# Scores in four row quarters, their banks shared with the products, and a rearranged order of work

## The chip, the cores and the metric

The kernel runs on one core of one Trainium2 chip. The metric is device time in microseconds for one execution of the whole program; lower is better. The engines are named as the profile names them: PE (TensorE matmuls) and PEld (its weight loads), DVE (VectorE), ACT (ScalarE), POOL (GpSimd) and SP (SyncE, which issues most DMAs).

## What is computed

The reference takes x of shape (4, 2048, 512) through four residual steps: a causal linear attention (layer a), a quantized product (ffn), a gated decaying recurrence (layer b), and the same ffn again. The change lies in layer b. Cut to what matters there:

```python
x = x + attn_a(layernorm(x))
x = x + ffn(layernorm(x))          # int8 levels of x and rhs, product, scales
x = x + attn_b(layernorm(x))
x = x + ffn(layernorm(x))

def attn_b(x):                     # 16 heads, rank 16, head width 32
    q, k, v = split(x @ q_w.T), split(x @ k_w.T), split(x @ v_w.T)
    q, k = rope(q), rope(k)
    q_r, k_r = q @ Wq, k @ Wk      # per head, 32 -> 16
    g = sigmoid(x @ g_w.T + g_b)
    # per step t: M = M * decay + outer(g_t * k_t * scale, v_t);  y_t = q_t @ M
    h = x + Y @ out_w.T + out_b
    return layernorm(h) * ln_g + ln_b
```

The recurrence is computed in chunks of 128 rows. Inside a chunk the outputs are masked scores (a product of decayed queries and keys) times v; what comes from earlier chunks goes through a stored state.

## The kernel before

Layer a comes first, and then layer b with the last ffn (`layer_b_mild`; the other branch is not taken with these inputs). Layer b walks over 32 blocks of 256 rows. A block has two rows of 128 tokens (index i) and two groups of eight heads (index g, 16 ranks for each head, so 128 partitions), which makes four chunks: chunk c is row c // 2, group c % 2.

The order of the work on PE, DVE, ACT and POOL is written out by hand in `blocks_of(n)`, under `tc.manual_schedule`: each engine runs its instructions in the order of the program. SP is not among these engines, so the order of its DMA queue is left to the framework. One call of `blocks_of(n)` interleaves four blocks: the chunks of block B (n), the products that prepare `after` (n + 1), the loading, normalization and turning of the rows of `later` (n + 2), and the output normalization and ffn of `before` (n - 1).

A chunk has two functions. `scores` (L1318) multiplies keys `k1` and queries `q1`: the 128 partitions are cut in two halves of 64 (four heads each), and each half gives a score bank of 128 x 512, four heads beside each other. The queries are laid out with one copy for each of the four heads, zero outside the head's own 16 partitions; ACT makes these copies in `prepare` (L1294) from `qs`. `scores` then issues the state's part of the outputs (`pyT`, L1333) and the masks (L1339), by which DVE copies the scores out of PSUM with the causal triangle. The second function holds `update` (`pub`, L1360, then `pairs` on DVE and the state on POOL) and `outputs` (`pyT`, L1373, and ACT's copy to `yT`).

The other functions that the change and the steps of the prediction touch:

- `features` (L1230) makes the rotated queries or keys of one group: 8 f32 products into `pr`, which DVE reads twice (`xc`, `xs`, L1238).
- `gates` (`pg`), `keys` (`pl`, L1263; then q by ACT, k by DVE) and `values` (`pvb`; the copy `vb` by ACT, L1212).
- `prepare`: on DVE `k1` (L1282; the page prints it as k) and `qs` (L1288), on ACT the head copies, on POOL `ke` and `q0` (L1298).
- `turn_keys`: `turn_halves` copies `ke` on DVE (`planes`, L710) and issues a DMA transpose from SP (L712). `turned_keys` joins the result on ACT (`kt`, L717).
- `norm_row` and `turn_row`: the same for the rows of a later block; `turn_row` has two POOL additions (L1205, L1206).
- `project` (`py`, L1394) and `weigh_output` (`h` by DVE at L1398, then statistics); `norm_output` (`h` at L131, then two POOL instructions).
- `levels` quantizes for the ffn; its product (`pf`, L681) is read by DVE (`f_y`, L683) and added by POOL (L684); `store` writes the block out.

PSUM has eight banks. In layer b they are handed out in rings, each used in turn:

```python
bank = banks(psum, mm=3, s=2, y=2, u=1)
```

"mm" serves pr, pg, pl, pvb, pf and py; "s" the scores. A tile that comes to a place in its ring waits until the last reader of the tile before it there is done. P is 128, TB 256, NTB 2, QB 128, NQ 1, R 16 and HG 8, so the loop over j in `scores` runs once.

Of the kernel before, what the change touches and what calls it, by code (L numbers as in the profile page):

```python
# [10 lines left out]
F32 = mybir.dt.float32  # L11
BF16 = mybir.dt.bfloat16
U16 = mybir.dt.uint16
AF = mybir.ActivationFunctionType
# [32 lines left out]
def hybrid_block_kernel(ctx: ExitStack, tc: tile.TileContext, t: dict, out: bass.AP):  # L47
# [588 lines left out]
    def run(steps):  # L636
        for f in steps:
            f()
# [432 lines left out]
    def layer_b_mild():  # L1071
        with ExitStack() as es:
# [4 lines left out]
            w = es.enter_context(tc.tile_pool(name="mb_w", bufs=1, reuse_waits="tile"))  # L1077
            pool = es.enter_context(tc.tile_pool(name="mb", bufs=2, reuse_waits="tile"))
            psum = es.enter_context(tc.tile_pool(name="mb_ps", bufs=1, space=PSUM, reuse_waits="tile"))

            bank = banks(psum, mm=3, s=2, y=2, u=1)
            at = [(b, blk) for b in range(NB) for blk in range(SEQ // TB)]

            def load_x(n):
# [23 lines left out]
            for name in ("b_gb", "b_decay", "head4", "diag", "causal"):  # L1108
# [167 lines left out]
            def prepare(B, g):  # L1276


                q, k = B.qk[g]
                A = Block()  # L1280
                A.k1 = pool.tile([P, NTB, NQ, P], F32, name=f"k1{g}", bufs=1)
                nc.vector.tensor_tensor(  # L1282
                    A.k1,
                    k.rearrange("p (i s) -> p i s", s=P).unsqueeze(2).to_broadcast([P, NTB, NQ, P]),
                    tk[:, g, :, :].unsqueeze(1).to_broadcast([P, NTB, NQ, P]), ALU.mult,
                )
                qs = pool.tile([P, NTB * NQ, QB], F32, name="qs", bufs=1)
                nc.vector.tensor_tensor(  # L1288
                    qs, q.rearrange("p (j s) -> p j s", s=QB),
                    tq[:, g, :].unsqueeze(1).to_broadcast([P, NTB * NQ, QB]), ALU.mult,  # L1290
                )
                A.q1 = pool.tile([P, NTB * NQ, 4, QB], F32, name=f"q1{g}", bufs=1)
                for h in range(4):
                    nc.scalar.activation(A.q1[:, :, h, :], qs, AF.Copy, scale=small["head4"][:, h : h + 1])  # L1294
# [18 lines left out]
            def chunk(B, i, g):  # L1313
# [4 lines left out]
                def scores():  # L1318


                    A = B.prep[g]
                    ps = [bank([P, NQ, 4, QB], F32, name="ps", tag="s") for _ in range(2)]
                    for j in range(NQ):
                        for half in range(2):
                            r = slice(half * 64, (half + 1) * 64)
                            nc.tensor.matmul(  # L1326
                                ps[half][:, j, :, :], A.k1[r, i, j, :], A.q1[r, NQ * i + j, :, :],
                                start=True, stop=True,
                            )
                    C.py = [bank([P, P], F32, name="pyT", tag="y") for _ in range(2)]  # L1330
                    for half in range(2):
                        r = slice(half * 64, (half + 1) * 64)
                        nc.tensor.matmul(  # L1333
                            C.py[half], st[r, half * P : (half + 1) * P], A.q0[r, i, :],
                            start=True, stop=False, skip_group_check=True,
                        )
                    C.a = pool.tile([P, 2, 4, P], F32, name="ab")
                    for half in range(2):
                        nc.vector.tensor_tensor(  # L1339
                            C.a[:, half, :, :].rearrange("p h (j s) -> p h j s", s=QB),  # L1340
                            ps[half].rearrange("p j h s -> p h j s"),
                            small["causal"].rearrange("p (j s) -> p j s", s=QB).unsqueeze(1)
                            .to_broadcast([P, 4, NQ, QB]),
                            ALU.mult,
                        )


# [20 lines left out]
                def outputs():  # L1368

                    for half in range(2):  # L1370
                        for h in range(4):
                            lo = g * HG * DB + (4 * half + h) * DB
                            nc.tensor.matmul(  # L1373
                                C.py[half][h * DB : (h + 1) * DB, :], B.v[:, i, lo : lo + DB],
                                C.a[:, half, h, :], start=False, stop=True, skip_group_check=True,
                            )
# [11 lines left out]
                return (lambda: (scores(), zero())) if ends else scores, lambda: run([outputs] if ends else [update, outputs])  # L1388

            def project(B, i):  # L1390

# [4 lines left out]
            def weigh_output(B, i):  # L1396
                h = B.h[i] = pool.tile([P, D], F32, name="h")
                nc.vector.tensor_tensor(h, B.py.pop(i), B.xr[:, i, :], ALU.add)  # L1398
                B.stats[i] = stats(pool, h.unsqueeze(1), 1)

            def norm_output(B, i):
                h, x = B.h.pop(i), B.x[:, i, :]
# [52 lines left out]
            def blocks_of(n):  # L1455
                B, after, later = blocks.get(n), blocks.get(n + 1), blocks.get(n + 2)
                before = blocks.get(n - 1)
                nothing = lambda: None
                chunks = [chunk(B, c // G, c % G) if B else (nothing, nothing) for c in range(2 * G)]


                if B:
                    turned_keys(B, 0)
                chunks[0][0]()
                if before:
                    weigh_ffn(before, 0)
                if after:
                    run(features(after, "q", 0))
                chunks[0][1]()
                if later:  # L1470
                    weigh_row(later, 0)
                if before:
# [8 lines left out]
                    turned_keys(B, 1)  # L1481
                chunks[1][0]()
                if before:
                    weigh_output(before, 1)
                if after:
                    run(gates(after, 0) + keys(after, 0))
                chunks[1][1]()
                if before:
                    run(before.levels[0])
                if later:  # L1490
# [3 lines left out]
                if later:  # L1494
                    weigh_row(later, 1)
                if after:
                    run(features(after, "q", 1))


                chunks[2][0]()  # L1500
                if after:
                    prepare(after, 0)
                if before:
                    weigh_ffn(before, 1)
                if later:
                    turn_row(later, 0)
                if after:
                    run(values(after, 0))
                    turn_keys(after, 0)
                chunks[2][1]()  # L1510
                if later:
                    norm_row(later, 1)
                if before:
                    levels(before, 1)
                if after:
# [25 lines left out]
            def tail(B):  # L1541
# [24 lines left out]

                project(B, 1)
                weigh_ffn(B, 0)
                weigh_output(B, 1)
                quantize(0)  # L1570
                norm_last(B, 1)
# [21 lines left out]
def _constants(seq):  # L1593
# [13 lines left out]
        "head4": (p[:, None] // R % 4 == np.arange(4)[None, :]).astype(f),  # L1607
# [89 lines left out]
```

## Time and profile before

| what | value |
|---|---|
| median of 3 runs | 3969.62 us (3968.38 to 3970.84) |
| the profiled execution, its own time | 3970.43 us |
| its span, first to last instruction | 3968.6 us |
| mean granted TensorE clock | 0.992 |
| PE busy, DVE, POOL, ACT | 98%, 61%, 38%, 22% of the span |
| score matmuls ps (L1326) | 144.5 us busy, 512 instructions |
| masks ab (L1339) | 164.1 us busy, 256 instructions |
| head copies q1 (L1294) | 109.2 us busy, 256 instructions |
| one block of layer b, score to score | 45.74 us |

An f32 matmul shows as two instructions, one for each pass. A line of a group gives the busy time in us, the mean of one instruction in ns, and the idle time of the engine just ahead of it with what ended most of that. A line of the timeline gives the start and the length in us, the instruction, how many were merged, and in brackets the idle time before and its releaser. [...]work on PE is better measured from start to start.

### The profile page before, as it was taken

The numbers are of one execution on the slowest core, as the hardware profiler recorded it, in microseconds if no ns is written. First come the engines' busy times: TensorE is split into PE (matmuls) and PEld (weight loads), VectorE is DVE, ScalarE is ACT, GpSimd is POOL, SyncE is SP. The second block draws the span as 40 slices with busy tenths as digits, with TensorE's granted clock in tenths as the row PEclk, the third lists the DMA queues.
The fourth block names the chain that finished last, engine by engine and source line by source line (L and its number), as shares of the span: only waits on it lengthen the run. The fifth ranks groups of instructions, "written<-read, shape, count | busy, mean of one in ns | idle before, by whom it ended". The sixth has DMA issues, their size and how long they took to land.

```text
span 3968.6 us, 53472 instructions
## 1 busy us (share of the span) xinstructions
PE 3886.1 (98%) x20765; PEld 2128.6 (54%) x20765; DVE 2418.3 (61%) x4552; ACT 879.2 (22%) x1550; POOL 1504.4 (38%) x2523
## 2 busy tenths in 40 slices
PE   7999999999999999999999996999999999999997
PEld 4555554555545555555555553666666666666664
DVE  4455555555555555554554554677777777777776
ACT  1221221221221221221222211222222222222221
POOL 3223323323233233233233223355555545555553
PEclk9999999999999999999999997999999999999999
DMA  4122222222212212212212214122212222222211
GB/s 139 30 41 54 67 41 54 67 40 54 67 39 55 67 39 55 67 39 55 67 39 55 57 29 144 23 54 54 55 50 51 52 53 54 55 50 51 53 37 32
DMA packets 430967, 216.97 MB, mean 55 GB/s; under 512 B 362736, under 2 KB 375920, under 8 KB 430704
## 3 DMA queue, kind: packets, MB, share of 16 engines
q1 hardware_dynamic: 429584, 211.89, 21.9%
q8 instruction: 165, 2.70, 0.3%
q10 hardware_dynamic: 1120, 1.57, 0.1%
q14 instruction: 98, 0.80, 0.1%
HBM read 91.49 MB, written 34.08 MB: 32 GB/s over the span
## 4 chain that ended last, share of the span: by engine, by line
PE 95%; DMA 2%; DVE 2%; POOL 1%; issue 0%; ACT 0%; SPq 0%; ACTq 0%; DVEq 0%; POOLq 0%
PE pr L1230 12%; PE pk L648 11%; PE pq L648 11%; PE pv L648 11%; PE po L648 11%; PE pvb L648 6%; PE py L1394 5%; PE pss L888 3%; PE ps L1326 3%; PE pn L974 3%; PE pg L648 3%; PE pl L1263 3%; PE pf L681 3%; PE pn L968 3%; PE pu L904 2%; PE pyT L1373 1%
## 5 line engine op out<-in xcount | busy, mean ns | idle before, releaser
L648 PE MATMUL pq<-xnTa,a_Wq 128*128 128x512 f32 x1024 | 492.2, 608 | 0.0
L648 PE MATMUL pk<-xnTa,a_Wk 128*128 128x512 f32 x1024 | 491.0, 604 | 0.0
L648 PE MATMUL pv<-a_Wv,xnTa 128*128 128x512 f32 x1024 | 476.6, 604 | 2.9 <-ACT xnTa L141 2.9
L648 PE MATMUL po<-a_Wo_sb,oT 128*128 128x512 f32 x1024 | 467.4, 601 | 7.2 <-DVE oT L950 7.1
L126 POOL TENSOR_SCALAR rs<-mv 128x1 f32<-128x1 f32 x320 | 82.3, 257 | 1019.4 <-DVE mv L125 1016.3
L914 POOL TENSOR_TENSOR within<-state,u 64x64 f32<-64x64 f32 x256 | 158.1, 618 | 523.4 <-ACT u L909 513.8
L648 PEld LDWEIGHTS po<-a_Wo_sb,oT 128*128 128x128 f32 x1024 | 189.3, 190 | 236.0 <-issue 220.0
L648 PEld LDWEIGHTS pv<-a_Wv,xnTa 128*128 128x128 f32 x1024 | 188.8, 191 | 234.4 <-issue 224.2
L648 PEld LDWEIGHTS pq<-xnTa,a_Wq 128*128 128x128 f32 x1024 | 181.4, 189 | 193.1 <-issue 182.8
L648 PEld LDWEIGHTS pk<-xnTa,a_Wk 128*128 128x128 f32 x1024 | 184.5, 189 | 180.9 <-issue 158.8
L909 ACT COPY u<-pu 128x256 f32<-128x256 f32 x128 | 47.7, 373 | 1026.9 <-PE pu L904 1026.9
L1230 PE MATMUL pr<-xnTb,m_kT_sb 128*128 128x256 f32 x1024 | 237.9, 385 | 0.0
L894 DVE TENSOR_TENSOR sm<-pss,causal 128x512 f32<-128x512 f32 x256 | 164.2, 683 | 119.8 <-PE pss L888 119.8
L1230 PE MATMUL pr<-xnTb,m_qT_sb 128*128 128x256 f32 x1024 | 237.2, 385 | 0.0
L717 ACT COPY kr<-turned 128x1024 uint16<-128x1024 uint16 x120 | 139.3, 1161 | 426.3 <-DMA turned<-planes 426.3
L648 PE MATMUL pvb<-b_vT_sb,xnTb 128*128 128x512 f32 x512 | 233.7, 599 | 0.0
L1394 PE MATMUL py<-b_oT_sb,yT 128*128 128x512 f32 x512 | 231.1, 594 | 0.0
L1339 DVE TENSOR_TENSOR ab<-ps,m_causal 128x512 f32<-128x512 f32 x256 | 164.1, 682 | 95.4 <-PE ps L1326 95.4
L1230 PEld LDWEIGHTS pr<-xnTb,m_qT_sb 128*128 128x128 f32 x1024 | 193.7, 192 | 32.6 <-ACT q L1294 0.2
L683 DVE SCALAR_TENSOR_TENSOR f_y<-pf,f_sc,rscale 128x512 f32<-128x512 f32 x126 | 94.5, 750 | 191.2 <-PE pf L681 191.0
L1230 PEld LDWEIGHTS pr<-xnTb,m_kT_sb 128*128 128x128 f32 x1024 | 189.4, 190 | 35.6 <-issue 12.3
L127 POOL TENSOR_TENSOR rs<-rs,neg_half 128x1 f32<-128x1 f32 x320 | 194.0, 607 | 26.3
(171 smaller groups left out, 6302.8 us busy)
## 6 DMA issues: line engine op xcount, KB each, us to landing
wide<-rec SPq DMA_DIRECT2D x124, 256.0 KB, 3.6
mmid<-xa SPq DMA_DIRECT2D x16, 1024.0 KB, 4.3
out<-xb SPq DMA_DIRECT2D x31, 512.0 KB, 2.8
xa<-in_x SPq DMA_DIRECT2D x15, 1024.0 KB, 6.6
xb<-mmid SPq DMA_DIRECT2D x30, 512.0 KB, 3.8
turned<-planes SPq DMA_TRANSPOSE x304, 3.1
m_cos<-in_cos SPq DMA_DIRECT2D x30, 128.0 KB, 2.5
m_sin<-in_sin SPq DMA_DIRECT2D x30, 128.0 KB, 2.3
```

What stands on the lines that cost most here:

```text
L127: nc.gpsimd.tensor_tensor(rs, rs, neg_half[:, :n], ALU.pow)
L648: nc.tensor.matmul(held[0], lhs(), rhs(), start=(n == 0), stop=(n == len(pairs) - 1))
L681: nc.tensor.matmul(pf, qT[:, c, :], rq[:, c, :], start=(c == 0), stop=(c == KC - 1))
L717: nc.scalar.copy(dst.bitcast(U16).rearrange("p n (t two) -> p n t two", two=2), turned.rearrange("p (two n) t -> p n t two", two=2),)
L888: nc.tensor.matmul(ps[h][:, i, :], k[r, chunks[i]], q[r, chunks[i]], start=True, stop=True)
L894: nc.vector.tensor_tensor(s, ps[h], causal.unsqueeze(1).to_broadcast([P, NTA, P]), ALU.mult)
L914: nc.gpsimd.tensor_tensor(A.before[i + 1][r, r], A.before[i][r, r], u[r, i, :], ALU.add)
L968: nc.tensor.matmul(pn[:, i, :], A.before[i], q[:, chunks[i]], start=(i == 0), stop=False, skip_group_check=True,)
L974: nc.tensor.matmul(pn[r, i, :], v()[:, i, vh[h]], A.sm[h][:, i, :], start=False, stop=True, skip_group_check=True,)
L1230: nc.tensor.matmul(pr[:, half, :], wp[name][:, c, lo : lo + P], B.xnT[:, c, :], start=(c == 0), stop=(c == KC - 1),)
L1339: nc.vector.tensor_tensor(C.a[:, half, :, :].rearrange("p h (j s) -> p h j s", s=QB), ps[half].rearrange("p j h s -> p h j s"), small["cau ...
L1394: nc.tensor.matmul(py, B.yT[i][:, c, :], wo[:, c, :], start=(c == 0), stop=(c == KC - 1))
```

## The change

The scores are cut in four quarters of 32 partitions (two heads each) instead of two halves: four matmuls of 256 columns, each into a bank of its own, 128 x 256. `q1` holds two copies instead of four. The masks become four DVE instructions of 256 columns, in a function of their own (`mask`) that comes behind `scores`. The rings "mm" (3) and "s" (2) become one of five, from which the scores take four places in turn. `weigh_output` is cut in two: `add_output`, which empties the bank of `py`, is put ahead of the masks in chunks 1 and 3. In `blocks_of` further pieces change place: `features(after, "q", 1)` and `values(after, 0)` are exchanged; `norm_row(later, 1)` goes right behind the third chunk's masks and `weigh_ffn`, ahead of that chunk's outputs; `prepare(after, 0)` goes from chunk 2 to chunk 3, ahead of its gates; and `turn_keys(after, 0)` goes to the end of chunk 3, ahead of `prepare(after, 1)`.

```diff
-            bank = banks(psum, mm=3, s=2, y=2, u=1)
+            ring = banks(psum, mm=5, y=2, u=1)
+            def bank(shape, dtype, name, tag):
+                return ring(shape, dtype, name, "mm" if tag == "s" else tag)
...
-                for h in range(4):
-                    nc.scalar.activation(A.q1[:, :, h, :], qs, AF.Copy, scale=small["head4"][:, h : h + 1])
+                A.q1 = pool.tile([P, NTB, 2, P], F32, name=f"q1{g}", bufs=1)
+                for h in range(2):
+                    nc.scalar.activation(A.q1[:, :, h, :], qs, AF.Copy, scale=small["head2"][:, h : h + 1])
...
-                    ps = [bank([P, NQ, 4, QB], F32, name="ps", tag="s") for _ in range(2)]
-                    for j in range(NQ):
-                        for half in range(2):
-                            r = slice(half * 64, (half + 1) * 64)
-                            nc.tensor.matmul(
-                                ps[half][:, j, :, :], A.k1[r, i, j, :], A.q1[r, NQ * i + j, :, :],
-                                start=True, stop=True,
-                            )
+                    C.ps = [bank([P, 2, P], F32, name="ps", tag="s") for _ in range(HG // 2)]
+                    for n in range(HG // 2):
+                        r = slice(n * 2 * R, (n + 1) * 2 * R)
+                        nc.tensor.matmul(C.ps[n], A.k1[r, i, :], A.q1[r, i, :, :], start=True, stop=True)
...
+                def mask():
+                    C.a = pool.tile([P, HG, P], F32, name="ab")
+                    for n in range(HG // 2):
+                        nc.vector.tensor_tensor(
+                            C.a[:, 2 * n : 2 * n + 2, :], C.ps[n],
+                            small["causal"].unsqueeze(1).to_broadcast([P, 2, P]), ALU.mult,
+                        )
...
+            def add_output(B, i):
                 h = B.h[i] = pool.tile([P, D], F32, name="h")
                 nc.vector.tensor_tensor(h, B.py.pop(i), B.xr[:, i, :], ALU.add)
-                B.stats[i] = stats(pool, h.unsqueeze(1), 1)
+
+            def weigh_output(B, i):
+                B.stats[i] = stats(pool, B.h[i].unsqueeze(1), 1)
...
                 chunks[1][0]()
                 if before:
+                    add_output(before, 1)
+                chunks[1][1]()
+                if before:
                     weigh_output(before, 1)
...
                 if after:
-                    run(features(after, "q", 1))
+                    run(values(after, 0))
                 chunks[2][0]()
-                if after:
-                    prepare(after, 0)
+                chunks[2][1]()
                 if before:
                     weigh_ffn(before, 1)
                 if later:
                     turn_row(later, 0)
-                if after:
-                    run(values(after, 0))
-                    turn_keys(after, 0)
-                chunks[2][1]()
                 if later:
                     norm_row(later, 1)
+                if after:
+                    run(features(after, "q", 1))
+                chunks[2][2]()
...
                 chunks[3][0]()
                 if B:
+                    add_output(B, 0)
+                chunks[3][1]()
+                if B:
                     weigh_output(B, 0)
                 if after:
+                    prepare(after, 0)
                     run(gates(after, 1) + keys(after, 1))
-                chunks[3][1]()
+                chunks[3][2]()
                 if before:
                     run(before.levels[1])
                     store(before)
                 if later:
                     turn_row(later, 1)
                 if after:
+                    turn_keys(after, 0)
                     prepare(after, 1)
```

More of the change, by code (lines that the diff above doesn't have):

```diff
@@ L1107, in layer_b_mild @@
             small = {}
-            for name in ("b_gb", "b_decay", "head4", "diag", "causal"):
+            for name in ("b_gb", "b_decay", "head2", "diag", "causal"):
                 small[name] = w.tile(list(t[name].shape), F32, name=f"m_{name}")
@@ L1280, in prepare @@
                 A = Block()
[L1281 to L1285, printed above, removed]
-                )
[L1287 to L1292, printed above, removed]
-                for h in range(4):
-                    nc.scalar.activation(A.q1[:, :, h, :], qs, AF.Copy, scale=small["head4"][:, h : h + 1])
+                A.k1 = pool.tile([P, NTB, P], F32, name=f"k1{g}", bufs=1)
+                qs = pool.tile([P, NTB, P], F32, name="qs", bufs=1)
+                for dst, src, tab in ((A.k1, k, tk[:, g, 0, :]), (qs, q, tq[:, g, :])):
+                    nc.vector.tensor_tensor(
+                        dst, src.rearrange("p (i s) -> p i s", s=P),
+                        tab.unsqueeze(1).to_broadcast([P, NTB, P]), ALU.mult,
+                    )
+                A.q1 = pool.tile([P, NTB, 2, P], F32, name=f"q1{g}", bufs=1)
+                for h in range(2):
+                    nc.scalar.activation(A.q1[:, :, h, :], qs, AF.Copy, scale=small["head2"][:, h : h + 1])
                 A.ke = pool.tile([P, NTB, P], F32, name="ke", bufs=1)
@@ L1321, in scores @@
                     A = B.prep[g]
-                    ps = [bank([P, NQ, 4, QB], F32, name="ps", tag="s") for _ in range(2)]
-                    for j in range(NQ):
-                        for half in range(2):
-                            r = slice(half * 64, (half + 1) * 64)
-                            nc.tensor.matmul(
-                                ps[half][:, j, :, :], A.k1[r, i, j, :], A.q1[r, NQ * i + j, :, :],
-                                start=True, stop=True,
-                            )
+                    C.ps = [bank([P, 2, P], F32, name="ps", tag="s") for _ in range(HG // 2)]
+                    for n in range(HG // 2):
+                        r = slice(n * 2 * R, (n + 1) * 2 * R)
+                        nc.tensor.matmul(C.ps[n], A.k1[r, i, :], A.q1[r, i, :, :], start=True, stop=True)
                     C.py = [bank([P, P], F32, name="pyT", tag="y") for _ in range(2)]
@@ L1336, in scores @@
                         )
-                    C.a = pool.tile([P, 2, 4, P], F32, name="ab")
-                    for half in range(2):
+                def mask():
+                    C.a = pool.tile([P, HG, P], F32, name="ab")
+                    for n in range(HG // 2):
                         nc.vector.tensor_tensor(
[L1340 to L1344, printed above, removed]
+                            C.a[:, 2 * n : 2 * n + 2, :], C.ps[n],
+                            small["causal"].unsqueeze(1).to_broadcast([P, 2, P]), ALU.mult,
                         )
@@ L1374, in outputs @@
                                 C.py[half][h * DB : (h + 1) * DB, :], B.v[:, i, lo : lo + DB],
-                                C.a[:, half, h, :], start=False, stop=True, skip_group_check=True,
+                                C.a[:, 4 * half + h, :], start=False, stop=True, skip_group_check=True,
                             )
@@ L1386, in outputs @@
                         )
-                return (lambda: (scores(), zero())) if ends else scores, lambda: run([outputs] if ends else [update, outputs])
+                return (lambda: (scores(), zero())) if ends else scores, mask, lambda: run([outputs] if ends else [update, outputs])
             def project(B, i):
@@ L1394, in project @@
                     nc.tensor.matmul(py, B.yT[i][:, c, :], wo[:, c, :], start=(c == 0), stop=(c == KC - 1))
-            def weigh_output(B, i):
+            def add_output(B, i):
                 h = B.h[i] = pool.tile([P, D], F32, name="h")
                 nc.vector.tensor_tensor(h, B.py.pop(i), B.xr[:, i, :], ALU.add)
-                B.stats[i] = stats(pool, h.unsqueeze(1), 1)
+            def weigh_output(B, i):
+                B.stats[i] = stats(pool, B.h[i].unsqueeze(1), 1)
             def norm_output(B, i):
@@ L1458, in blocks_of @@
                 nothing = lambda: None
-                chunks = [chunk(B, c // G, c % G) if B else (nothing, nothing) for c in range(2 * G)]
+                chunks = [chunk(B, c // G, c % G) if B else (nothing, nothing, nothing) for c in range(2 * G)]
                 if B:
@@ L1464, in blocks_of @@
                 chunks[0][0]()
+                chunks[0][1]()
                 if before:
@@ L1468, in blocks_of @@
                     run(features(after, "q", 0))
-                chunks[0][1]()
+                chunks[0][2]()
                 if later:
@@ L1486, in blocks_of @@
                     run(gates(after, 0) + keys(after, 0))
-                chunks[1][1]()
+                chunks[1][2]()
                 if before:
@@ L1568, in tail @@
                 weigh_ffn(B, 0)
+                add_output(B, 1)
                 weigh_output(B, 1)
@@ L1606, in _constants @@
         "diag": (p[:, None] // R == np.arange(HG * DB)[None, :] // DB).astype(f),
-        "head4": (p[:, None] // R % 4 == np.arange(4)[None, :]).astype(f),
+        "head2": (p[:, None] // R % 2 == np.arange(2)[None, :]).astype(f),
         "sin2": np.ascontiguousarray(
```

## The prediction

> **What bounds the kernel now.** I read the page first, then the stage table over one block of layer b, then the timeline around the end of a block. The change lies in layer b, whose 32 blocks of 256 rows run from about 2506 us on.
>
> ```profile
> PE 3886.1 (98%) x20765; PEld 2128.6 (54%) x20765; DVE 2418.3 (61%) x4552; ACT 879.2 (22%) x1550; POOL 1504.4 (38%) x2523
> ...
> PE 95%; DMA 2%; DVE 2%; POOL 1%; issue 0%; ACT 0%; SPq 0%; ACTq 0%; DVEq 0%; POOLq 0%
> ...
> L1339 DVE TENSOR_TENSOR ab<-ps,m_causal 128x512 f32<-128x512 f32 x256 | 164.1, 682 | 95.4 <-PE ps L1326 95.4
> ```
> ```profile
> 3004.24:3049.98 45.74, 45.74 (x282) 28.22 (x281) 34.62 (x63) 11.12 (x27) 24.55 (x31) 1.00 0.21 53
> ```
>
> TensorE carries 95% of the chain. In the stage table the second number is PE's busy time: all 45.74 of 45.74 us, at full clock. So a microsecond saved on PE is a microsecond won unless a wait replaces it, and any new PE wait costs its full length. The other engines have room (DVE 34.6, POOL 24.6, ACT 11.1), so only their order can hurt. The mask row is the reader of the score banks: DVE idles 95.4 us in all before it, waiting for the scores, so it is usually ahead of PE.
>
> ```profile
> 3020.62 0.60 PE L1263 MATMUL pl<-xs_q,low_q 128*64 128x256 f32 x4
> 3021.05 0.60 PE L1263 MATMUL pl<-xc_k,low_k 128*64 128x256 f32 x4
> 3021.49 0.60 PE L1263 MATMUL pl<-xs_k,low_k 128*64 128x256 f32 x4
> 3022.02 0.32 PE L1360 MATMUL pub<-vb,kt 128*32 128x64 f32 x8
> ```
>
> Here the reader sees two prices. An f32 matmul is two passes, and neighbouring tiles run together: four instructions take 0.435 us, so a pass of 256 columns is 0.2155. Where the tile form changes (128*64 to 128*32) the next start comes after 0.53, not 0.435: 0.095 for the switch.
>
> ```profile
> 3046.65 0.75 DVE L683 SCALAR_TENSOR_TENSOR f_y<-pf,f_sc,rscale 128x512 f32<-128x512 f32 x1 [0.57 <-PE pf L681]
> 3047.32 0.41 DVE L1282 TENSOR_TENSOR k<-k,tk 128x256 f32<-128x256 f32 x1
> 3047.48 1.38 POOL L684 TENSOR_TENSOR xb<-xb,f_y 128x512 f32<-128x512 f32 x1 [0.60 <-DVE f_y L683]
> 3047.65 1.49 DVE L1288 TENSOR_TENSOR qs<-q,tq 128x256 f32<-128x256 f32 x1
> ...
> 3048.82 1.45 POOL L1205 TENSOR_TENSOR xb<-xb,b_ln_b_row 128x512 f32<-128x512 f32 x1
> ...
> 3049.06 1.49 DVE L131 TENSOR_SCALAR h<-h,mv,rs 128x512 f32<-128x512 f32 x1
> ...
> 3049.24 1.71 ACT L1294 ACTIVATE q<-qs,m_head 128x256 f32<-128x256 f32 x4 [2.14 <-DVE qs L1288]
> ...
> 3049.98 1.13 PE L1326 MATMUL ps<-q,k 64*128 64x512 f32 x4
> ...
> 3050.85 0.56 ACT L1212 COPY vb<-pvb 128x512 f32<-128x512 f32 x1
> 3050.94 0.39 PE L1333 MATMUL pyT<-q,state_b 64*128 64x128 f32 x4
> ...
> 3051.26 3.72 PE L1230 MATMUL pr<-xnTb,m_qT_sb 128*128 128x256 f32 x16
> ```
>
> This is the place that decides. `qs` has k1's shape but takes 1.49 instead of 0.41: it stands until POOL's addition ends at 3048.86 and finishes 0.28 later; `h` does the same behind the next POOL addition. In this stretch each such DVE instruction costs one POOL instruction. The ACT copy of `vb` comes behind the four head copies, so at 3050.85, though its product ended at about 3050.05. That costs nothing now: the next `pr` takes another bank.
>
> **The change part by part.** S is the start of a block's first score matmul, 3049.98 here.
>
> *Scores on PE.* Before, ps to pyT is 0.96 and pyT to the next product 0.32: 1.28. The sixteen `pr` passes last 3.65 (3051.26 to 3054.91) = 16 x 0.2155 + 0.095 + 0.107; the last term is the first weight load, exposed after a switch. After: load 0.107, two passes of 256 columns, all four quarters together (0.431), switch from 32-row to 64-row form 0.095: 0.633. Then pyT: its load is now exposed (0.107), two passes of 128 columns (0.109 each), switch 0.095: 0.42. Sum 1.05, saving 0.235 per chunk. That the quarters overlap is taken from the nearest row: the 32-column tiles of `pub` and `pyT` run four at once, and the two 64-row halves of `ps` run together.
>
> Two rules of the skill speak against it. The Trainium skill, "TensorEngine Tiling (Array Packing)", Tiling Modes: a change of tiling mode, not of tile, drains the array. No row shows 32-row to 64-row; rows show it for other forms (0.53 above), so I take it. Without a drain and reload here the saving is 0.235 + 0.20 = 0.435; with it 0.235. And "TensorE: Matmul & The Clock Gate", Measured speedup vs the span model: four row tiles gave 3.07x, not 4x. Then a pass of four costs 0.2155 x 4/3.07 = 0.28, the saving is 0.235 - 2 x 0.065 = 0.105. The rows of this trace (pairs of 64-row tiles: 0.43 per 512-column pass, as a single one) show no such loss, so I use 0.235.
>
> *Masks.* Two of 512 elements (0.68 each in the page's L1339 row, issued 0.60 apart) become four of 256. Bounds: half of 0.60, or the whole. The nearest pair, k<-pl (256, 0.43) and f_y (512, 0.75), suggests 0.33 apart: 1.36 instead of 1.28 per chunk. DVE has 11 us free per block and the outputs come 4 us after the scores; hidden. Four waits instead of two on the score matmuls: from nothing to 0.03, in the range.
>
> *Head copies.* ACT does two instead of four: 0.8 us less ahead of `vb`. k1 and qs keep their size (QB is 128, NQ is 1).
>
> *The ring.* mm goes from three banks to five and takes the scores in. A block allocates 30, so places are fixed and each waits for the tile five before. Walked through: the fourth score of chunk 1 waits for the k features' eviction (xs_k ends S+12.5); pg in chunks 1 and 3 for py, which add_output, now ahead of the masks, empties 0.2 in time; q features of half 1 for `vb` of half 0, with 0.25 to spare (ACT idle there). The one that fails: the q features in chunk 0 take the bank of values(after, 1), five before, and so wait for the `vb` copy.
>
> *Moves.* Features q 1 and values 0 change places on PE: nothing, same work. norm_row(later, 1) goes ahead of chunk 2's outputs: its DVE copy and SP transpose earlier, landing before turn_row needs it. prepare(after, 0) goes into chunk 3: two DVE (0.41 each), two ACT, two POOL instructions (0.65 each), into the 1.67 us in which DVE waited there for q. turn_keys(after, 0) goes from chunk 2 to behind f_y: one DVE copy (0.41 to 0.84) and one SP transpose. On SP it meets the store, which waits for POOL's L684 (3048.86); the transpose lands near S+2.4, before pub at S+5 needs it.
>
> *The wait.* DVE: f_y ends 3047.40. `planes` takes k1's free slot (3047.32 to 3047.73). k1 then stands where qs stood, to 3049.14; qs where h stood, to 3050.55, 1.41 later than now. ACT: first head copy 3050.65, two at 0.40, `vb` 3051.46 to 3052.02, PE 0.05 later: q features at S+2.09, instead of S+1.28 now and S+1.05 unhindered. Behind them wait pub, pyT and k features; DVE in chunk 0 is anyway bound to POOL's chain up to S+5.7, so nothing further slips, and the chunk 1 wait above is covered by this delay.
>
> *Sum per block.* Chunk 0: +0.81. Chunks 1 to 3: -3 x 0.235 = -0.705. Net +0.105. Blocks 2 to 30: 29 x 0.105 = +3.0. Blocks 0 and 1, whose predecessor has no f_y or too early a chain: 8 x -0.235 = -1.9. The last block and tail wait on DVE masks, not PE: 0. Score waits, 0.01 to 0.02 per chunk in 29 blocks: about +1.5. In all +2.6 on the profiled 3970.43 (span 3968.6); the median of the runs is 3969.62, 0.8 below, which gives 3972.2.
>
> **The rivals.** *No wait* (0.15): DVE slips k1 and qs in ahead of POOL's addition; `vb` is copied at S+0.7 and PE starts at S+1.05. Then 0.235 x 4 x 31 = 29 minus about 2 for the chunk 1 wait: 3943. Against: qs did not slip in in this trace.
>
> *No drain* (0.10): 29 x (0.81 - 3 x 0.435) = -14, and -3.5 in blocks 0 and 1: 3952. For: both are row tilings. Against: every other change of form shows the 0.095.
>
> *The quarters' passes are longer* (0.12), ending slower: at 0.28 a pass the block is +0.81 - 0.315 = +0.5, x 29 = +14, less 0.8: 3983; with no overlap beyond pairs, 4010. It decides once a pass exceeds about 0.24: then three savings fall below 0.56 and the block loses over 0.25. For: the skill's 3.07x. Against: the overlap of the other tiles.
>
> *Small margins fail* (0.15): pg twice and pr once per block lie 0.2 to 0.25 from a wait; missing each by 0.15 to 0.25 is 29 x 0.45 to 0.75: 3980 to 3992.
>
> *My sum* (0.48): 3964 to 3980 on its own, nearly all of it within 0.2%.
>
> **How the numbers follow.** 0.2%, 8 us, is about what a measurement of this kernel can tell from no change. Faster: 0.15 + 0.10. Slower: 0.12 + 0.15 and 0.06 of my sum's upper end. Same: 0.42. From 3942 to 3992 the range takes in all but the worst overlap.
>
> **What would show it.** Right: chunk 0's `pr` starts near 2.1 us after the scores, waiting for ACT vb; other chunks at 1.05; `qs` twice stretched near 1.4; ps as eight short matmuls with starts 7 ns apart; period about 45.85. Wrong: no idle PE ahead of `pr`; pyT's weights loaded during ps; score passes over 0.24; a PE wait ahead of pg.

## The result and the profile after

The changed kernel takes 3975.7 us (median of 20 runs, 3973.55 to 3978.71), the kernel before 3969.62 (median of 20 runs, 3965.37 to 3971.49). The ratio is 1.0018, with a 95% interval from 1.0012 to 1.0024: slower by some 6 us, at the edge of the 0.2% that the prediction named as no change. The profiled execution took 3973.55 us, with a span of 3971.8: 3.2 more than the span before.

First the page, then the stage table over one block (columns: window, then its length, then busy time and instruction count of PE, PEld, DVE, ACT and POOL, then clock, DMA share and GB/s).

```profile
PE 3850.2 (97%) x21155; PEld 2119.4 (53%) x21277; DVE 2418.6 (61%) x4808; ACT 833.8 (21%) x1422; POOL 1510.1 (38%) x2523
...
PE 91%; DVE 4%; DMA 2%; issue 1%; ACT 1%; POOL 1%; SPq 0%; ACTq 0%; DVEq 0%; POOLq 0%
```
```profile
3002.99:3048.91 45.92, 44.64 (x296) 27.93 (x297) 34.56 (x71) 9.75 (x22) 24.70 (x31) 1.00 0.21 53
```

PE has less to do, and the kernel is longer. Before, PE was busy for all 45.74 us of a block; now for 44.64 of 45.92. Not all of the 1.28 us between is real: the page counts 122 fewer matmuls than weight loads (before, the counts were equal), and the groups of layer b by form show where some of these matmul records are missing:

```profile
L681 PE MATMUL pf<-rq,f_qT 128*128 128x512 bf16 x186 | 51.5, 387 | 10.2 <-issue 9.9 <-ACT yT L1375 0.4
...
L681 PEld LDWEIGHTS <-f_qT 128*128 128x128 bf16 x248 | 19.4, 98 | 28.0 <-issue 13.0 <-DMA f_qT<-f_q 0.8
```

248 loads and 186 products of the ffn: the 9.9 us "issue" ahead of `pf`, 0.32 in a block, is the place of records that are not in the trace. What is left is 0.96 us a block. PE's list of waits in layer b (columns: us in all, times, longest) says what it is:

```profile
PE pr L1234 <- ACT vb L1216: 27.9, 29, 1.0
...
PE pyT L1368 <- DVE ab L1337: 5.0, 3, 2.8
```

One wait, once in each of 29 blocks, is all that is regular (the `pyT` row belongs to the last block). The timeline around the end of a block shows its chain:

```profile
2999.67 0.75 DVE L683 SCALAR_TENSOR_TENSOR f_y<-pf,f_sc,rscale 128x512 f32<-128x512 f32 x1 [0.57 <-PE pf L681]
3000.34 0.42 DVE L710 COPY planes<-ke 128x512 uint16<-128x512 uint16 x1
3000.50 1.38 POOL L684 TENSOR_TENSOR xb<-xb,f_y 128x512 f32<-128x512 f32 x1 [0.59 <-DVE f_y L683]
3000.67 1.49 DVE L1288 TENSOR_TENSOR k<-k,tk 128x256 f32<-128x256 f32 x1
...
3001.84 1.45 POOL L1209 TENSOR_TENSOR xb<-xb,b_ln_b_row 128x512 f32<-128x512 f32 x1
...
3002.08 1.48 DVE L1288 TENSOR_TENSOR qs<-q,tq 128x256 f32<-128x256 f32 x1
...
3002.99 0.71 PE L1325 MATMUL ps<-q,k 32*128 32x256 f32 x8
3003.64 0.49 PE L1329 MATMUL pyT<-q,state_b 64*128 64x128 f32 x4
3003.66 0.91 ACT L1294 ACTIVATE q<-qs,m_head 128x256 f32<-128x256 f32 x2 [3.61 <-DVE qs L1288]
...
3004.48 0.56 ACT L1216 COPY vb<-pvb 128x512 f32<-128x512 f32 x1
3005.09 3.72 PE L1234 MATMUL pr<-xnTb,m_qT_sb 128*128 128x256 f32 x16 [0.96 <-ACT vb L1216]
```

`planes`, the copy of `turn_keys(after, 0)`, takes the last unhindered place behind `f_y`. k1 then stands to 3002.16, 0.28 after POOL's first addition, and `qs` to 3003.56, behind the second. The head copies, `vb` and the bank follow on ACT, and PE starts `pr` 2.10 us after the scores. Where nothing waits, in chunk 1, the same step is shorter:

```profile
3016.51 0.71 PE L1325 MATMUL ps<-q,k 32*128 32x256 f32 x8
3017.15 0.49 PE L1329 MATMUL pyT<-q,state_b 64*128 64x128 f32 x4
3017.58 1.99 PE L648 MATMUL pg<-xnTb,b_gT_sb 128*128 128x256 f32 x8
```

From scores to the next product it is 0.64 + 0.43 = 1.07 us; it was 1.28. Score to score, the four chunks are 13.52, 9.96, 12.49 and 9.96, and were 12.70, 10.18, 12.69 and 10.18: +0.82 and three times about -0.21.

The difference of the two spans, put together from the starts of the first scores of each block:

| part | after less before, us |
|---|---|
| up to the first score of layer b (2504.71, was 2506.27) | -1.56 |
| blocks 0 and 1 (40.36 and 44.89, were 40.76 and 45.74) | -1.25 |
| 29 blocks, 45.92 instead of 45.74 in nearly all | +5.1 |
| last block and tail (50.84, was 49.94) | +0.9 |
| sum | +3.2 |

The first row is not the change's: in the kernels below, whose program is the same up to there, layer b begins between 2503.7 and 2508.6. The others give +4.75, nearer to the difference of the medians. The fourth row hangs on the granted clock of this execution (see *The last block* below), so what the blocks ahead of it show is 5.1 less 1.25.

### The profile page after: what moved, and what is told of

Same layout as the page of the kernel before. It is cut to its first block, busy times and chain, and to the rows that moved or that the text cites. A ratio compares the mean times of both kernels' runs of the same rounds, so it can differ in the third digit from the quotient of the medians.

```text
span 3971.8 us, 54542 instructions
## 1 busy us (share of the span) xinstructions
PE 3850.2 (97%) x21155; PEld 2119.4 (53%) x21277; DVE 2418.6 (61%) x4808; ACT 833.8 (21%) x1422; POOL 1510.1 (38%) x2523
## 4 chain that ended last, share of the span: by engine, by line
PE 91%; DVE 4%; DMA 2%; issue 1%; ACT 1%; POOL 1%; SPq 0%; ACTq 0%; DVEq 0%; POOLq 0%
PE pr L1234 12%; PE pk L648 11%; PE pq L648 11%; PE pv L648 11%; PE po L648 11%; PE py L1389 5%; PE pss L888 4%; PE pn L974 3%; PE pg L648 3%; PE pl L1267 3%; PE pvb L648 3%; PE pn L968 3%; PE pf L681 3%; PE pu L904 2%; PE ps L1325 2%
## 5 line engine op out<-in xcount | busy, mean ns | idle before, releaser
L127 POOL TENSOR_TENSOR rs<-rs,neg_half 128x1 f32<-128x1 f32 x320 | 202.5, 633 | 26.3
L838 DVE TENSOR_TENSOR xa<-po,xa 128x512 f32<-128x512 f32 x64 | 44.1, 689 | 258.5 <-PE po L648 258.5
```

Source lines behind the costliest of these rows:

```text
L127: nc.gpsimd.tensor_tensor(rs, rs, neg_half[:, :n], ALU.pow)
```

## The experiments

The theory was that of the prediction: the quarters save PE time, and the place of `turn_keys(after, 0)` loses it again through DVE, ACT and one shared bank. The rivals: the time is lost in the quarters themselves, in the masks, or in the ring. In the table a usual block is the median of the 31 distances from one block's first score to the next one's. The results:

| kernel | median, us | ratio to before (95%) | usual block, us |
|---|---|---|---|
| after | 3975.7 | 1.0018 (1.0012 to 1.0024) | 45.92 |
| e1_vb_first | 3952.04 | 0.9958 (0.9941 to 0.9974) | 45.18 |
| e2_keys_early | 3947.42 | 0.9948 (0.9931 to 0.9965) | 45.00 |
| e3_old_order | 3989.42 | 1.0052 (1.0035 to 1.0069) | 46.30 |
| e4_halves | 3968.97 | 0.9999 (0.9990 to 1.0008) | 45.74 |
| e5_pool_late | 3956.26 | 0.9966 (0.9952 to 0.9980) | 45.29 |
| e6_exchange | 3983.85 | 1.0037 (1.0022 to 1.0051) | 46.24 |
| e7_state_quarters | 3942.19 | 0.9932 (0.9915 to 0.9948) | 44.87 |
| e8_best | 3944.54 | 0.9938 (0.9922 to 0.9955) | 44.89 |
| e9_both | 3941.54 | 0.9934 (0.9920 to 0.9947) | 44.71 |
| e10_norm_back | 3944.87 | 0.9937 (0.9923 to 0.9950) | 44.89 |

Beside these kernels, the kernel before took 3968.76, 3969.13 or 3968.54 us.

### e1_vb_first: `vb` ahead of the head copies

```diff
                     turn_keys(after, 0)
+                    run(values(after, 1))
                     prepare(after, 1)
...
                     turn_keys(after, 1)
-                    run(values(after, 1))
```

> The changed kernel with values(after, 1) moved ahead of prepare(after, 1), so that ACT copies vb before the two head copies; PE, DVE and POOL keep their order. Theory (the wait is ACT's queue: vb stands behind head copies whose qs is late, and the q features need its bank): the 0.96 us of idle PE ahead of the q features of chunk 0 goes, and they start about 1.07 us behind the scores; 29 x 1.0 = 29 us less, minus at most 0.3 a block for a new wait of chunk 1's fourth score on xs_k: 20 to 29 us below the changed kernel. Rival (the chain of DVE and POOL at the block's end is itself the bound, and the wait only shows at the features): PE waits later in chunk 0 or in chunk 1 instead, and the time stays within 5 us of the changed kernel.

3952.04 us, 23.7 below after. In its timeline `qs` is as late as in after, but ACT copies `vb` first, and `pr` starts 1.06 us behind the scores with no wait:

```profile
2996.62 0.71 PE L1325 MATMUL ps<-q,k 32*128 32x256 f32 x8
2996.72 0.58 ACT L1216 COPY vb<-pvb 128x512 f32<-128x512 f32 x1 [3.05 <-PE pvb L648]
2997.28 0.91 ACT L1294 ACTIVATE q<-qs,m_head 128x256 f32<-128x256 f32 x2
...
2997.68 3.72 PE L1234 MATMUL pr<-xnTb,m_qT_sb 128*128 128x256 f32 x16
...
3008.62 0.68 DVE L1242 TENSOR_TENSOR xs_k<-pr,m_sin 128x512 f32<-128x512 f32 x1
...
3009.10 1.01 PE L1325 MATMUL ps<-q,k 32*128 32x256 f32 x8
```

So the wait hung on ACT's order alone; late queries by themselves cost nothing. Part of the second wait forecast by the prediction comes up instead: the fourth quarter of chunk 1 waits 0.3 for the bank that `xs_k` empties (the scores of 0.71 take 1.01), and chunk 1 takes 10.25 instead of 9.96.

### e2_keys_early: `turn_keys(after, 0)` ahead of chunk 3's outputs

```diff
                     run(gates(after, 1) + keys(after, 1))
+                    turn_keys(after, 0)
                 chunks[3][2]()
...
                 if after:
-                    turn_keys(after, 0)
                     prepare(after, 1)
```

> The changed kernel with turn_keys(after, 0) moved from the end of chunk 3 to right behind keys(after, 1), into DVE's gap ahead of f_y. Theory (the copy planes takes the free slot ahead of POOL's addition, so k1 and qs each wait one POOL instruction): qs ends near 0.84 us ahead of the scores as before the change, the head copies and vb are done by 0.7 us behind them, the q features do not wait: 20 to 29 us below the changed kernel, about the same as with vb first. Rival (ACT is late for another reason, for instance the transposed keys' copy kt): the wait on vb stays at 0.9 us and the time within 3 us of the changed kernel.

3947.42 us, 28.3 below after and 0.5% below before. Only the place of one DVE copy of 0.42 us and its DMA differs from after. Its timeline:

```profile
3036.05 0.41 DVE L1288 TENSOR_TENSOR k<-k,tk 128x256 f32<-128x256 f32 x1
3036.39 1.49 DVE L1288 TENSOR_TENSOR qs<-q,tq 128x256 f32<-128x256 f32 x1
...
3038.71 0.71 PE L1325 MATMUL ps<-q,k 32*128 32x256 f32 x8
3038.82 0.59 ACT L1216 COPY vb<-pvb 128x512 f32<-128x512 f32 x1
...
3039.78 1.56 PE L1234 MATMUL pr<-xnTb,m_qT_sb 128*128 128x256 f32 x6
```

k1 has the free place again, `qs` waits for one POOL addition and not two, and ends before the scores start. This is what is lost in after: 0.92 us in each block (45.92 less 45.00), 26.7 in 29. The rival named above, that `kt` makes ACT late, would have left the wait on `vb` in place; it is gone.

### e3_old_order: the quarters and the ring in the order of before

Quarters, four masks and the ring of five stay; `blocks_of` has the order of before, with `add_output` behind the masks.

```diff
-                if before:
-                    add_output(before, 1)
                 chunks[1][1]()
                 if before:
+                    add_output(before, 1)
                     weigh_output(before, 1)
...
-                    run(values(after, 0))
+                    run(features(after, "q", 1))
...
+                if after:
+                    prepare(after, 0)
...
-                if later:
-                    norm_row(later, 1)
...
-                    run(features(after, "q", 1))
+                    run(values(after, 0))
+                    turn_keys(after, 0)
+                if later:
+                    norm_row(later, 1)
```

> The quarters, four masks and the ring of five alone: the order of the work is that of the kernel before, with add_output behind the masks where weigh_output was. Theory (ring places decide): pg in chunks 1 and 3 takes the bank of py, which is now emptied only behind four masks, near 2.8 us after the scores instead of being needed at 1.07: 1.7 us of idle PE twice in a block; and values(after, 0) waits some 0.3 us for xs_q: 29 x (3.7 - 0.84) = 83 us above the kernel before, 4040 to 4065. Rival (the rearranged order is what costs, the quarters and the ring are free): 20 to 28 us below the kernel before.

3989.42 us: slower, as expected in sign, but by far less than forecast. PE's waits and its timeline:

```profile
PE pvb L648 <- DVE xs_q L1242: 29.5, 31, 1.0
```
```profile
3025.15 1.99 PE L648 MATMUL pg<-xnTb,b_gT_sb 128*128 128x256 f32 x8
...
3026.01 0.68 DVE L1393 TENSOR_TENSOR h<-py,xr 128x512 f32<-128x512 f32 x1
...
3036.19 3.67 PE L648 MATMUL pvb<-b_vT_sb,xnTb 128*128 128x512 f32 x8 [0.99 <-DVE xs_q L1242]
```

`pg` starts while DVE has yet to read `py`, so it cannot stand in `py`'s bank, as "each tile waits for the one five before" had it. It lost only about 0.2 us, behind the first mask: it took the bank of the first score quarter. The bank addresses in the built program say the same: a place goes to the next tile in the order in which the last readers of the old tiles stand in the program, not in that of their allocation. The wait that does come is `pvb`'s for `xs_q`, 0.99 us in each block, right behind the q features on PE. So the exchange of `features(after, "q", 1)` and `values(after, 0)` is what takes this wait away (e6).

### e4_halves: what the quarters are worth by themselves

e2, with the scores in two halves again, so with four head copies and two masks. Four places of the ring are still taken, two of them unused, so that the other tiles keep theirs.

```diff
-                for h in range(2):
-                    nc.scalar.activation(A.q1[:, :, h, :], qs, AF.Copy, scale=small["head2"][:, h : h + 1])
+                for h in range(4):
+                    nc.scalar.activation(A.q1[:, :, h, :], qs, AF.Copy, scale=small["head4"][:, h : h + 1])
...
-                    C.ps = [bank([P, 2, P], F32, name="ps", tag="s") for _ in range(HG // 2)]
-                    for n in range(HG // 2):
-                        r = slice(n * 2 * R, (n + 1) * 2 * R)
+                    C.ps = [bank([P, 4, P], F32, name="ps", tag="s") for _ in range(4)]
+                    C.ps = [C.ps[0], C.ps[3]]
+                    for n in range(2):
+                        r = slice(n * 64, (n + 1) * 64)
```

> As e2 (turn_keys early), with the scores in two halves of 64 rows again, four head copies and two masks; four places of the ring are still taken in each chunk, two of them unused, so that every product keeps its place. It prices the quarters alone. Theory (a quartered score stage saves 0.21 us on PE a chunk): 31 x 4 x 0.21 = 26 us above e2, near the kernel before; the later vb (two more head copies, 0.8 us) may add up to 0.3 us a block. Rival (the quarters' own saving is eaten by the added switch or by skew): within 5 us of e2.

3968.97 us, no different from before, and 21.6 above e2. The block is 45.74 against e2's 45.00. The quarters are worth 4 x 0.21 = 0.84 us a block, less 0.1 that e2 waits in chunk 1. Ring and order by themselves are worth nothing; they make the room for the quarters.

### e5_pool_late: POOL's two additions moved away

After, with the two POOL additions of `turn_row(later, 1)` behind `norm_output` (a new function `add_rows`).

```diff
                 if later:
-                    turn_row(later, 1)
+                    turn_row(later, 1, late=True)
...
                     (norm_output if after else norm_last)(B, 0)
+                if later:
+                    add_rows(later, 1)
```

> The changed kernel with the two POOL additions of turn_row(later, 1) moved behind norm_output's two POOL instructions; DVE, ACT and PE keep their order. Theory (a DVE instruction with two SBUF inputs stands until the POOL instruction that runs beside it is done): k1 still waits for L684, but qs then stands only behind the 0.65 us ke and ends near 0.2 us ahead of the scores instead of 0.57 behind them; vb ends near 1.3 us, the wait ahead of the q features shrinks from 0.96 to 0.1 to 0.4 us: 15 to 25 us below the changed kernel. Rival (DVE is late by its own extra copy of 0.41 us, POOL only runs beside it): qs stays within 0.2 us of where it was, and the time within 5 us of the changed kernel.

3956.26 us, 19.4 below after. `planes` keeps its bad place, k1 is stretched as before by POOL's L684, but `qs` behind it no longer meets an addition of 1.45 us:

```profile
2996.52 1.49 DVE L1292 TENSOR_TENSOR k<-k,tk 128x256 f32<-128x256 f32 x1
...
2997.69 0.82 POOL L1302 TENSOR_TENSOR ke<-k,down 128x256 f32<-128x256 f32 x1
2997.93 0.86 DVE L1292 TENSOR_TENSOR qs<-q,tq 128x256 f32<-128x256 f32 x1
...
3000.32 3.72 PE L1238 MATMUL pr<-xnTb,m_qT_sb 128*128 128x256 f32 x16 [0.33 <-ACT vb L1220]
```

`qs` beside a POOL instruction of 0.82 takes 0.86, and the wait for `vb` falls from 0.96 to 0.33 us. The length of the DVE instruction follows that of its neighbour on POOL, so the stretch comes from POOL and does not belong to `qs`. Two inputs are not needed for it: `h` (L131), with one tile as input, takes 1.49 beside an addition of 1.45 in after, and 0.54 where POOL is idle (in e2, at 3015.74).

### e6_exchange: e3 with one move of the change

```diff
-                    run(features(after, "q", 1))
+                    run(values(after, 0))
...
-                    run(values(after, 0))
+                    run(features(after, "q", 1))
```

> The old order with quarters and the ring of five (e3), and one move of the rearranged order added: features(after, q, 1) and values(after, 0) exchanged. Theory (a bank goes to the next product in the order in which its last reader stands in the program, and in e3 values(after, 0) got that of the q features computed just before it): the 0.99 us wait of pvb on xs_q goes, 31 times: 29 us below e3, near 3960; a wait of 0.15 to 0.25 us for the first mask stays in chunks 1 and 3. Rival (the wait only moves, to the q features, now right behind the scores, waiting for vb): within 10 us of e3.

3983.85 us, only 5.6 below e3 where 29 were expected from the wait that goes. `pvb` waits no more; the wait moved on:

```profile
PE ps L1325 <- DVE xs_k L1242: 15.4, 29, 0.6
```
```profile
3037.15 1.29 DVE L710 COPY planes<-ke 128x512 uint16<-128x512 uint16 x1
...
3044.04 0.68 DVE L1242 TENSOR_TENSOR xs_k<-pr,m_sin 128x512 f32<-128x512 f32 x1
...
3044.87 0.67 PE L1325 MATMUL ps<-q,k 32*128 32x256 f32 x2 [0.56 <-DVE xs_k L1242]
```

The last score quarter of chunk 3 takes the bank of the k features, and DVE is late with it. In chunk 2 DVE still has `prepare(after, 0)` and `turn_keys(after, 0)` ahead of it, whose `planes` takes 1.29 there. The other three quarters have run when the last one may start, so it runs alone: another 0.6 us to the state's product. Chunk 3 takes 11.17 us instead of 9.96. The move of those two pieces out of chunk 2 so has a likely use in after, and only the new place of one of them is bad; no run moves them alone, so this is not shown.

### e7_state_quarters: does the drain go if state and scores have the same rows?

e2, with the state's product in four tiles of 32 rows and 64 columns.

```diff
-                    for half in range(2):
-                        r = slice(half * 64, (half + 1) * 64)
+                    for n in range(HG // 2):
+                        r = slice(n * 2 * R, (n + 1) * 2 * R)
+                        c = slice(n % 2 * 64, n % 2 * 64 + 64)
                         nc.tensor.matmul(
-                            C.py[half], st[r, half * P : (half + 1) * P], A.q0[r, i, :],
+                            C.py[n // 2][c, :], st[r, n * 64 : (n + 1) * 64], A.q0[r, i, :],
```

> As e2 (turn_keys early), with the state's product in four tiles of 32 rows and 64 columns instead of two of 64 rows and 128 columns: the same 128 columns stream, but there is no change from 32-row to 64-row tiles behind the scores. It prices that change. Theory (every change of the tile form costs 0.095 us and an exposed weight load, the column number counting too): from the state product to the next product 0.38 instead of 0.43, 128 x 0.05 = 6 us below e2. Rival (only a change in the rows costs): 0.15 to 0.2 us a chunk, 19 to 26 us below e2. It is also possible that the eight small tiles overlap badly: then above e2.

3942.19 us, 5.2 below e2; the block is 44.87, 0.13 less. As single runs of e2 lie up to 7 us apart, the block says more than the median.

```profile
3005.12 0.88 PE L1325 MATMUL ps<-q,k 32*128 32x256 f32 x8
3005.93 0.45 PE L1330 MATMUL pyT<-q,state_b 32*64 32x128 f32 x8
3006.31 1.99 PE L648 MATMUL pg<-xnTb,b_gT_sb 128*128 128x256 f32 x8
```

From state to the next product it is 0.38 instead of 0.43. The state's weight loads, of 64 columns instead of 128, print 0.13 us instead of 0.18, and the second pass follows the first after 0.16 instead of 0.21. But the state product still starts about 0.30 us behind the start of the last score pass, which is 0.2155 for the pass and 0.09 on top: the same rows with another number of columns cost the switch as well. (This chunk's scores have the 0.1 us wait of e2 in them.)

### e8_best, e9_both and e10_norm_back

e8 is e2 with two more edits: DVE gets to `xs_k` earlier in chunk 0, and in the last block the masks stand ahead of `add_output`, as in before. e9 is e8 with e7's state tiles. e10 is e8 with `norm_row(later, 1)` put back behind chunk 2's outputs.

```diff
-                if later:
-                    weigh_row(later, 0)
...
                     run(features(after, "k", 0))
+                if later:
+                    weigh_row(later, 0)
...
                 chunks[3][0]()
+                if not after:
+                    chunks[3][1]()
                 if B:
                     add_output(B, 0)
-                chunks[3][1]()
+                if after:
+                    chunks[3][1]()
```

The same is done around `add_output(before, 1)` in chunk 1; the lines are left out here.

> As e2, with weigh_row(later, 0) moved behind the k features of chunk 0, and in the last block, where no product needs py's bank, the masks ahead of add_output. Theory (chunk 1's fourth score waits 0.1 us for xs_k, which stands behind 0.9 us of statistics): that wait goes, 29 x 0.1 = 3 us, and the last block wins about 1 us: 3 to 5 us below e2. Rival (the masks of chunk 1 or the quantized row then come late): no gain, or some us above e2.

> e8 with the state's product in four tiles of 32 rows and 64 columns (e7) as well. Theory (the two act at different places on PE and add up: e8 has no wait left in a block of 44.89 us, e7 takes 0.05 us off each of four chunks): a block of 44.70, 128 x 0.05 = 6 us below e8, near 3938. Rival (with PE earlier, a wait comes back, most likely chunk 1's fourth score on xs_k): within 2 us of e8.

> e8 with norm_row(later, 1) back behind chunk 2's outputs, where the kernel before has it; it prices that piece of the rearranged order alone. Theory (DVE's order in chunk 2 decides when xs_k is done, which the fourth score of chunk 3 waits for): its scaling and its copy, 1.2 us now, then stand between pairs and the levels, beside POOL's two additions, and take up to 3; xs_k, now about 2 us ahead of the scores of chunk 3, ends between 1 us ahead and 0.5 us behind: 0 to 15 us above e8. Rival (it has no part in any wait): within 2 us of e8.

e8: 3944.54 us, 2.9 below e2. Its chunks are 12.49, 9.96, 12.49 and 9.96, so no wait is left in a usual block. Of the 1 us expected from the last block nothing came: with the tail it takes 49.71, and took 49.77 in e2. In its second chunk the outputs now wait 1.01 us for the masks instead of 1.60, but `pf` behind them then waits 0.80 for its transposed input instead of 0.19.

e9: 3941.54 us, 0.66% below before (interval 0.53% to 0.80%), with the shortest usual block of all, 44.71 where 44.70 was forecast. By its stage table PE is busy for the whole of it again:

```profile
2982.50:3027.21 44.71, 44.71 (x316) 27.54 (x318) 33.49 (x72) 9.84 (x22) 24.53 (x30) 1.00 0.22 54
```

Only 3.0 us below e8 were found where 6 were expected. In the profiled execution the last block and tail of e9 take 52.43 us, 2.7 more than in e8, with a lower clock (see *The last block*). The runs of e7, e8 and e9 overlap, so that the medians do not rank these three.

e10 is the same as e8 in time and block: 3944.87 us and 44.89. What the move of `norm_row` changes is a margin:

```profile
3031.59 0.68 DVE L1242 TENSOR_TENSOR xs_k<-pr,m_sin 128x512 f32<-128x512 f32 x1
...
3032.50 0.71 PE L1325 MATMUL ps<-q,k 32*128 32x256 f32 x8
```

`xs_k` ends 0.2 us before chunk 3's scores start; in e8 it is 1.9 us before them. With e8's order the move of `norm_row`, for all its place in the change's name, buys no time.

## Why the prediction was right, and where it was not

*The wait* was the deciding step, and it came as forecast: `pr` 2.10 us behind the scores (2.09 forecast), in 29 blocks, with k1 and `qs` both stretched to near 1.49. e1 shows the ACT link (take `vb` ahead of the copies, and the wait is gone with `qs` as late as ever), e5 the POOL link, e2 the cause in the order.

*The scores on PE.* Forecast 0.633 to the state's product and 0.42 from it on; measured about 0.64 and 0.43. The saving was mis-sized by a tenth, 0.21 and not 0.235 per chunk. A part is in the sum itself: 1.28 less 0.633 and 0.42 is 0.227. For the rest, the starts of the four quarters lie 7 ns apart, as the signs named in the prediction had it, while its working had all four at once: 3 x 7 = 21 ns more than covers it. With 0.82 lost in chunk 0 and three savings of 0.21 the block grows by 0.18 and not by 0.105, which makes 5.1 us in the 29 blocks instead of 3.0. Blocks 0 and 1 gave 1.25 of the forecast 1.9, for the same reason and for a wait that the working did not have: in block 0 `pg` waits 0.41 us, once, for `xs_k`.

*The switch* was taken at 0.095 for a pair of forms that no row showed, and the rival without it would have given 3952. The state's product starts about 0.305 us behind the start of the last score pass, so it exists, as the Trainium skill's "TensorEngine Tiling (Array Packing)", Tiling Modes, led one to expect. The other rule, the 3.07x of "TensorE: Matmul & The Clock Gate", Measured speedup vs the span model, was rightly set aside: a pass of 0.28 would have put the state's product 0.13 us later than it is.

*Score waits.* The 1.5 us forecast for the masks' additional waits was not found: between 2600 and 3900 us PE's waits are that on `vb` and the missing records ahead of `pf`, and nothing else. That term and the too large saving offset each other, so by luck the sum came out closer than its terms.

*The last block* was costed at nothing, and took 0.9 more in the profiled execution. `add_output` now stands in front of its masks, and in this block DVE is the engine that PE waits for, so that order is the obvious suspect. The runs speak against it: e2 has the same order and takes 49.77 us from the block's first score to the end of the span, e8 with the masks first 49.71, and e10 and e9, also with the masks first, 50.95 and 52.43. What differs is the granted clock. The stage rows of the last block's second chunk, score to score, for before, after, e2, e8 and e10:

```profile
3925.12:3930.38 5.26, 3.43 (x38) 1.48 (x37) 4.39 (x11) 0.53 (x2) 0.65 (x2) 1.00 0.12 25
3927.32:3933.82 6.50, 4.44 (x41) 1.92 (x41) 4.79 (x14) 0.53 (x2) 1.48 (x3) 0.74 0.11 23
3899.30:3904.85 5.55, 3.76 (x42) 1.66 (x41) 4.73 (x13) 0.53 (x2) 0.64 (x2) 1.00 0.13 27
3897.82:3903.38 5.56, 3.76 (x41) 1.66 (x40) 4.83 (x13) 0.53 (x2) 0.51 (x2) 1.00 0.13 27
3901.03:3907.44 6.41, 4.61 (x42) 1.78 (x41) 4.83 (x13) 0.53 (x2) 1.36 (x3) 0.82 0.12 23
```

At clock 1.00 this chunk takes about 5.55 us with either order of the masks; at a mean of 0.74 or 0.82 it takes 6.4 to 6.5. In after its `pf` products start 0.43 us apart, in e2 0.22. This chunk alone is 1.24 longer than before, more than the whole 0.9; before has such a dip too, but later (0.50 from 3942.63 to 3945.63). What lowered the clock there, and whether the change has a part in it, stays open.

*The ring.* The rule of the working, that each tile waits for the one five before, gave the right answer for `pr` behind `vb`, and a false one for `pg` behind `py` in e3. "`pg` in chunks 1 and 3 for `py`, with 0.2 in time" was therefore the wrong reason for `add_output`'s move, and the rival of small margins rested partly on it. It did not come about: in after neither `pg` nor the fourth score waits in a usual block.

*SP.* The transpose of `planes` went ahead of the store and not behind it; nothing hung on that.

Open is where the rest of the 6 us between the medians comes from. The blocks ahead of the last one account for 3.85 (5.1 less 1.25). The clock in the last block, the scatter of the runs and the start of layer b can each add to it, and only one execution of each kernel was traced.

## What to carry to other kernels

When an instruction is moved, price the place it takes in the queue, not its length: here a copy of 0.42 us cost 28 us in all, because it used up the one place in which DVE runs unhindered, and the delay then went through ACT's order into a bank that PE needed. When products and their readers come to share one ring, follow each tile to the reader that empties its place, and put that reader ahead of work that is merely next in order on its engine (e1 moves one line for 24 us). A saving on the bounding engine should be measured apart from the rearrangement that makes room for it: only e2 against e4 showed that the quarters were worth 22 us that the whole change did not show.

## What was not expected of the hardware

- A switch of tile form costs its 0.09 us also where only the number of columns changes (32x128 to 32x64 in e7); equal rows do not save it.
- Four row quarters do not start together: 7 ns lie between their starts, so that a group of four is 21 ns longer than a single pass.
- A DVE instruction of 0.41 us took 1.49 beside a POOL addition of 1.38 or 1.45, and 0.86 beside one of 0.82 (e5): it ends about 0.28 us after POOL's instruction, with one input tile (`h`) as with two (`qs`). Beside POOL's small instructions of 128x1 it is not stretched (`qs` takes 0.42 in after, at 3042.14).
- In the last block of some executions the granted clock fell below 1.00 for a few microseconds: 0.74 over 6.50 us in after, against 1.00 over 5.55 us in e2.
